# A graph layer and an expert layer in one kernel: one-hot tables from dst rows on ACT, and block results kept in DRAM until the edges are done

## The chip, the cores and the metric

The kernel runs on one core of a Trainium2 chip. The metric is the device time of one execution in microseconds (us), as the median of several runs. The core has five engines that matter here: PE (TensorE, matrix products; PEld is its weight load), DVE (VectorE), ACT (ScalarE), POOL (GpSimd) and SP (SyncE, which only issues DMAs). Each engine works through its own instructions in the order in which the program lists them. An instruction that has to wait holds up all that stands behind it on its engine, DMA issues included.

## The reference, cut to what matters

There are 6250 nodes with 256 features and 100,000 edges that are sorted by destination (`dst`), denser towards low node numbers. First a graph attention layer with 8 heads and a feed-forward net of 1024 hidden values, then a layer of 8 experts of which each token (node) takes two:

```python
h = (xn @ W).reshape(N, HEADS, HEAD_DIM)
e = jax.nn.leaky_relu(a_src[src] + a_dst[dst], NEG_SLOPE)
emax = jax.ops.segment_max(e, dst, num_segments=N)
ee = jnp.exp(e - emax[dst])
denom = jax.ops.segment_sum(ee, dst, num_segments=N)
alpha = ee / denom[dst]
msg = h[src] * alpha[:, :, None]
agg = jax.ops.segment_sum(msg, dst, num_segments=N)
out = agg.reshape(N, HEADS * HEAD_DIM) + xn @ W_res + bias
out = layer_norm(out, ln2_g, ln2_b)
ff = gelu_tanh(out @ ffn_w1 + ffn_b1) @ ffn_w2 + ffn_b2
x = x + out + ff
...
xe = xn[None, :, :] * ln_g[:, None, :] + ln_b[:, None, :]
h = jax.nn.gelu(jnp.einsum('end,edh->enh', xe, W1) + b1[:, None, :], approximate=False)
y = jnp.einsum('enh,ehd->end', h, W2) + b2[:, None, :]
y_tok = jnp.transpose(y, (1, 0, 2))
sel = jnp.take_along_axis(y_tok, top_idx[:, :, None], axis=1)
x = x + (weights[:, :, None] * sel).sum(axis=1)
```

Everything is in float32.

## The kernel before, in words

**First stage.** For 49 tiles of 128 nodes the kernel computes the attention tables and writes them to DRAM: `tab_s` (row per node: h and factors of the source) and `tab_q` (factors of the destination, 32 nodes in a row).

**Edges.** The edges are cut into tiles of 128. A step takes four tiles (G = 4), one from each of four windows; each window holds dst nodes of a range of 32. One to eight steps with the same windows are a group. There are 196 steps and 110 groups, and they run from the last nodes to the first (`order`, L285). A step passes through stages (`STAGES`, L910), each of which works a fixed number of steps behind the first:

- `fetch` (L806, step s): four indirect DMAs from POOL gather 4 x 128 rows of `tab_s` by source into `gs`.
- `spread` (L817, s): DVE compares each edge's place in its window with 0 to 31 and so makes the one-hot table `oh` (edge by node). At a group's first step it also makes `qd`, the factors of the group's 128 nodes in block-diagonal form, by multiplying `gd` with the constant `quad`.
- `turn_spread` (L832, one step later): PE transposes `oh` into the PSUM tile `pt`, and ACT copies it to `oht` (node by edge). `pt` has one buffer and is also used by `turn` (L960), which transposes the nets' inputs.
- `give` (L839, two steps later): PE multiplies `oht` with `qd`: each edge gets the factors of its destination, in `pz`.
- `weigh` (L846, three later): DVE makes the messages `msg` from `gs` and `pz`.
- `add_tiles` (L860, four later): PE sums the messages by node into `pl` with `oh` as weights; at a group's end ACT copies `pl` to `part`.
- `place` (L884, a group's end): DVE makes `oh2`, which shifts the group's 128 nodes to their place in two tiles of nodes; `add_nodes` (L891) multiplies with it on PE, and `sum_up` (L898) adds the product on DVE.

`fetch_nodes` (L787) gathers the destination factors of 32 groups at once, writes them to `tab_g` in DRAM and reads them back as `gd`, turned.

**Work beside the edges.** Between the stages of each step a planner (`run_tasks`, L937) puts tasks of the rest: 25 node units of two tiles (division by the sum, layer norm, net, residual, router) and blocks of the expert layer. A task has an engine and an estimated cost in us. A step has room on each engine (`ROOM`, L64), less what the edges need themselves (`EDGES`, `BEHIND` at a group's end); a task is put in when its engine has room left, and what it needs was put in one step or more before. PE's room beside edges is so 7.5 - 1.3 = 6.2. After the edges `ROOM_AFTER` holds. Tasks are made while less than 40 us (`QUEUE`) of PE work is waiting.

**Blocks.** When the router has done with a chunk of four node tiles, `rank` and `enlist` (L1274, L1298) give each token a slot in its experts' lists, and `scatter` (L1347) writes its normed row to `xs` by indirect DMAs from POOL. A block is 256 tokens of one expert. There are 53 (and some more that run only if needed). Which expert and where it starts is read from the lists at run time, and a block can be planned when the lists are sure to hold it (`sure`, L1387: tokens so far, times two, less 255 for each of the 8 experts, over 256). The last chunk is the single tile of the first 128 nodes. For a block SP loads the rows (`load_block`, L1401) and 2 MB of weights (`load_weights`, L1390, two buffers); `net` (L996) is 16 products `ph` with eight Gelu on ACT (`up`, L977) and 16 products `py` (`down`, L987), on PE with a cost of 15.4 us. `finish` (L1424) adds the bias on DVE into `yb` (two buffers), `weigh_block` (L1430) multiplies with the router's weights on ACT, and `give_back` (L1435) adds 2 x 128 rows to the output tensor in DRAM by two indirect DMAs from POOL. `note` (L1413) copies the rows' token numbers to `to` (three buffers).

`store_new` (L1091) writes the node units' rows to the same output tensor from SP. The framework puts a wait wherever two instructions touch the same tensor and one of them writes: each scatter-add waits for the landing of the one before.

The main loop is at L1483.

Of the kernel before, what the change touches and what calls it, by code (L numbers as in the profile page):

```python
# [40 lines left out]
F32 = mybir.dt.float32  # L42
# [22 lines left out]
EDGES = {"PE": 1.3, "DVE": 2.0}  # L65
BEHIND = {"PE": 0.5, "DVE": 1.4}
ROOM_AFTER = {"PE": 7.7, "DVE": 7.0, "ACT": 7.0, "POOL": 5.2, "SP": 1e9}
# [151 lines left out]
def gnn_moe_kernel(  # L219
# [68 lines left out]
    NCW = -(-NW // P)  # L288
    DUMMY = NP
# [29 lines left out]
    xt_d = dp.tile([NT, P, KD * P], F32, name="xt_d")  # L319
    xs = dp.tile([E * CAP + BT, DX], F32, name="xs")  # L320

# [12 lines left out]
    snloc = gp.tile([P, NQ], F32, name="snloc")  # L334
    here = gp.tile([P, 2, NQ], F32, name="here")
# [55 lines left out]

    quad = cp.tile([P, G], F32, name="quad")
    nc.vector.memset(quad, 0.0)
    for j in range(G):
        nc.vector.memset(quad[j * W32:(j + 1) * W32, j:j + 1], 1.0)
# [52 lines left out]
    with ExitStack() as actx:  # L448
# [96 lines left out]
        nc.vector.tensor_copy(srf, srow)  # L545
        ends = ap_.tile([P, 2, NCH], F32, name="ends")
# [69 lines left out]
        for j in range(G):  # L616
            q = slice(j * W32, (j + 1) * W32)
            nc.vector.tensor_scalar(sn[q], first[q, :, j], pcol[q], float(-j * W32), op0=ALU.add,
                                    op1=ALU.add)
        nc.vector.tensor_sub(sn, sn, kff)  # L620
        nc.vector.tensor_scalar(snloc, sn, float(P), float(-P), op0=ALU.is_ge, op1=ALU.mult)
        nc.vector.tensor_add(snloc, snloc, sn)
        nc.vector.tensor_sub(sn, first[:, :, 0], kff)
# [45 lines left out]

        nc.vector.memset(acc_hi[:, NT - KHI, :], 0.0)  # L670
# [100 lines left out]
    GC = P // G  # L771
# [13 lines left out]
    gds = {}  # L785

    def fetch_nodes(c):  # L787

        gq = bw.tile([P, W32 * 2 * H], F32, name="gq", bufs=1)
        nc.gpsimd.indirect_dma_start(  # L790
            out=gq, out_offset=None, in_=tab_q,
            in_offset=bass.IndirectOffsetOnAxis(ap=qrow[:, c:c + 1], axis=0))
        nc.sync.dma_start(tab_g[c * P:(c + 1) * P, :], gq)
        n = min(GC, NQ - c * GC)
        gd = bw.tile([P, GC, 2 * H], F32, name="gd")
        nc.sync.dma_start(gd[:, :n], tab_g[c * P:c * P + n * G, :].rearrange(
            "(g j) (r c) -> (j r) g c", j=G, r=W32))
        gds[c] = gd
# [18 lines left out]
    def spread(s):  # L817

        q, i = order[s]
        oh = bw.tile([P, G, W32], F32, name="oh", bufs=6)  # L820
# [4 lines left out]
        if i == 0:  # L825
            qd = bw.tile([P, G, 2 * H], F32, name="qd", bufs=3)
            gd = gds[q // GC][:, q % GC, :]
            nc.vector.tensor_tensor(qd, gd[:, None, :].to_broadcast([P, G, 2 * H]),
                                    quad[:, :, None].to_broadcast([P, G, 2 * H]), op=ALU.mult)
            live[q, "qd"] = qd  # L830

    def turn_spread(s):  # L832
        po = cps.tile([P, KD, 2 * P], F32, name="pt")
        nc.tensor.transpose(po[:, 0, :P], live[s, "oh"].rearrange("p j r -> p (j r)"), ident)  # L834
        oht = bw.tile([P, P], F32, name="oht")
        nc.scalar.activation(oht, po[:, 0, :P], AF.Copy)  # L836
        live[s, "oht"] = oht

    def give(s):  # L839

        pz = bps.tile([P, G * 2 * H], F32, name="pz", bufs=2)
        nc.tensor.matmul(pz, live.pop((s, "oht")), live[order[s][0], "qd"].rearrange(
            "p j c -> p (j c)"), start=True, stop=True)
        live[s, "pz"] = pz
# [39 lines left out]
    def place(q):  # L884

        oh2 = bw.tile([P, P], F32, name="oh2")
        nc.vector.tensor_scalar(oh2, jrow[:, :P], snloc[:, q:q + 1], None, op0=ALU.is_equal)
# [10 lines left out]
    def sum_up(q):  # L898
# [4 lines left out]
        for b in range(2):  # L903
# [6 lines left out]
    STAGES = ((sum_up, 6), (weigh, 3), (add_tiles, 4), (place, 4), (turn_spread, 1), (give, 2),  # L910
              (spread, 0), (add_nodes, 5), (fetch, 0))
# [312 lines left out]
    ebi = rp.tile([P, NB], I32, name="ebi")  # L1224
    endi = rp.tile([P, E], I32, name="endi")
# [187 lines left out]
    def note(b, env):  # L1413

        x = env["xb"]
        to = cw.tile([P, 2], I32, name="to", bufs=3)
        nc.vector.tensor_copy(to, x.bitcast(I32)[:, :, D])
# [4 lines left out]
        env["to"], env["wt"] = to, wt  # L1422
# [12 lines left out]
    def give_back(j, env):  # L1435
        nc.gpsimd.indirect_dma_start(  # L1436
            out=out, out_offset=bass.IndirectOffsetOnAxis(ap=env["to"][:, j:j + 1], axis=0),
            in_=env["yb"][:, j, :], in_offset=None, compute_op=ALU.add, bounds_check=N - 1,
            oob_is_err=False)
# [11 lines left out]
    def block_unit(b, env):  # L1451
# [8 lines left out]
        g0 = task(lambda: give_back(0, env), "POOL", 2.6, [wb_])  # L1460
        stored.append(task(lambda: give_back(1, env), "POOL", 2.6, [g0]))
# [15 lines left out]
    EARLY = 10  # L1477
    final_list, there = [], None
    s, u, since, was_nodes = 0, 0, [], False

    with tc.manual_schedule():
        nc.sync.dma_start(xs[E * CAP:, :].rearrange("(p r) d -> p r d", r=2), blank[:, :2])
        while s < NG + LASTST or pending or u < len(units) or len(blocks) < NS:  # L1483
            for g in range(s, min(s + EARLY, NG)):
                if order[g][0] // GC not in gds:
                    fetch_nodes(order[g][0] // GC)
# [3 lines left out]
            if s == NG + LASTST:  # L1490
                edges.close()
            if len(firsts) < len(units) and len(firsts) <= s + 1:
# [32 lines left out]
            run_tasks(s, room)  # L1525
            s += 1
# [43 lines left out]
```

## Time and profile before

| | us |
|---|---|
| median of 3 runs | 2186.42 (2183.76 to 2202.97) |
| the profiled execution's own time | 1972.14 |
| its span, first to last instruction | 1970.4 |
| busy: PE / PEld / DVE / ACT / POOL | 1634.8 / 1250.6 / 1078.1 / 707.7 / 1122.1 |
| mean granted clock of TensorE | 0.926 |
| last gather of edge rows starts | 1569.0 |
| last list of tokens scattered | 1711.2 |
| DMA | 348.24 MB, mean 177 GB/s |

The profiled execution took 214 us less than the median of the runs. Lines of the profile have the form: line of the code, engine, operation, out<-in by the program's names, shapes, count, then busy time and mean of one in ns, then the idle time ahead of it and who ended it. In lines of waits three numbers follow: us in total, times, longest. "issue" is time for which the profile shows no releaser. In the chain of waits each line has a start, a length and what it was. Windows give the busy us of each engine in a stretch. Matmul ends are modelled, so a busy PE is not PE at its peak. The span has three stages: up to about 137 us the tables, then 196 edge steps with other work beside them, and from about 1577 us blocks alone.

### The profile page before, as it was taken

To read this page: it belongs to the slowest core of one execution; us is meant where nothing else is said; L and a number is where in the kernel's file an instruction comes from. 1 tells how busy PE (TensorE), PEld (TensorE's weight loads), DVE (VectorE), ACT (ScalarE), POOL (GpSimd) and SP (SyncE) were. 2 spreads that over 40 slices of the span, in tenths; PEclk is the share of its full clock that TensorE was granted. 3 is DMA by queue.
4 is the path that set the end of the run, shared out by engine and by line. 5 is a ranking of instruction groups with operands and counts; after the bars stand their busy time and mean duration, and the time that the engine had idled before them with its cause. 6 is when DMAs were issued, how large, how long until landed. Compare 5 with 4: busy or idle time off the path is not lost. (4 is left out here: it accounts for less than half of the span.)

```text
span 1970.4 us, 28382 instructions
## 1 busy us (share of the span) xinstructions
PE 1634.8 (83%) x8533; PEld 1250.6 (63%) x8533; DVE 1078.1 (55%) x3964; ACT 707.7 (36%) x1590; POOL 1122.1 (57%) x1165
## 2 busy tenths in 40 slices
PE   4835797778787988999899997996998949999997
PEld 3523565555555766766677765775776737777775
DVE  8836878877878775565667655462453501200000
ACT  3821232322233343344434342433334314333332
POOL 2027765655655767577778777777777722112122
PEclk8968899887887999999999998998999979999999
DMA  4967664644535456566564776576776655565652
GB/s 129 290 210 225 187 202 130 184 134 146 158 112 194 152 152 170 149 199 168 179 200 136 210 206 200 155 220 201 201 232 169 205 184 131 179 186 171 196 161 57
DMA packets 245260, 348.24 MB, mean 177 GB/s; under 512 B 46465, under 2 KB 200353, under 8 KB 245100
## 3 DMA queue, kind: packets, MB, share of 16 engines
q1 hardware_dynamic: 182476, 203.56, 31.8%
q0 software_dynamic: 59312, 139.32, 27.1%
q10 hardware_dynamic: 3312, 3.48, 0.6%
q8 instruction: 70, 1.15, 0.2%
q14 instruction: 90, 0.74, 0.1%
HBM read 282.90 MB, written 67.66 MB: 178 GB/s over the span
## 5 line engine op out<-in xcount | busy, mean ns | idle before, releaser
L812 POOL DMA_INDIRECT gs<-tab_s,srce x784 | 809.9, 1033 | 363.9 <-issue 198.9
L981 PE MATMUL ph<-turned_in,w1b 128*128 128x256 f32 x1696 | 400.3, 390 | 51.2 <-ACT ht L984 38.2
L991 PE MATMUL py<-w2b,ht 128*128 128x256 f32 x1696 | 382.6, 384 | 11.7 <-DVE lg L1121 6.2
L981 PEld LDWEIGHTS ph<-turned_in,w1b 128*128 128x128 f32 x1696 | 305.2, 193 | 124.4 <-ACT ht L984 57.4
L991 PEld LDWEIGHTS py<-w2b,ht 128*128 128x128 f32 x1696 | 325.0, 193 | 58.4 <-DVE lg L1121 7.7
L1436 POOL DMA_INDIRECT out_dram<-yb,to x106 | 176.9, 1668 | 312.5 <-ACT yb L1432 124.5
L984 ACT ACTIVATE ht<-ph,pc 128x256 f32<-128x256 f32 x424 | 198.4, 473 | 206.1 <-PE ph L981 205.6
L854 DVE TENSOR_TENSOR msg<-gs,msg 128x1024 f32<-128x1024 f32 x196 | 240.5, 1227 | 6.7
L1426 DVE TENSOR_TENSOR yb<-py,b2b 128x512 f32<-128x512 f32 x53 | 36.6, 690 | 360.4 <-PE py L991 276.8
L991 PE MATMUL py<-w_sb,ht 128*128 128x256 f32 x784 | 190.5, 405 | 17.3 <-DVE lg L1121 15.0
L981 PE MATMUL ph<-turned_in,w_sb 128*128 128x256 f32 (+1 forms) x800 | 192.5, 394 | 14.2 <-ACT ht L984 14.2
L991 PEld LDWEIGHTS py<-w_sb,ht 128*128 128x128 f32 x784 | 158.7, 205 | 46.4 <-DVE lg L1121 19.6
L981 PEld LDWEIGHTS ph<-turned_in,w_sb 128*128 128x128 f32 x800 | 150.4, 200 | 44.6 <-ACT ht L984 20.3
L873 ACT ACTIVATE part<-pl 128x264 f32<-128x264 f32 x110 | 42.9, 390 | 322.3 <-PE pl L869 319.6
L836 ACT ACTIVATE oht<-pt 128x128 f32<-128x128 f32 x196 | 53.9, 275 | 271.5 <-PE pt L834 214.8
L869 PE MATMUL pl<-msg,oh 128*32 128x264 f32 x1568 | 130.9, 406 | 17.1 <-DVE msg L854 17.0
L1351 POOL DMA_INDIRECT xs<-xe,slot x98 | 103.4, 1055 | 54.3 <-DMA xs<-blank 22.1
L894 PE MATMUL p<-part,oh 128*128 128x264 f32 x220 | 84.3, 469 | 59.5 <-DVE acc_hi L905 38.8
L984 ACT ACTIVATE ht<-ph,prm 128x256 f32<-128x256 f32 (+1 forms) x200 | 92.2, 469 | 113.0 <-PE ph L981 112.6
L834 PEld LDWEIGHTS pt<-ident,oh 128*128 128x128 f32 x196 | 27.6, 141 | 138.3 <-issue 81.0
L834 PE MATMUL pt<-ident,oh 128*128 128x128 f32 x196 | 65.5, 334 | 49.6 <-ACT turned_in L973 23.1
L973 ACT ACTIVATE turned_in<-pt,pc 128x256 f32<-128x256 f32 x106 | 53.9, 559 | 134.4 <-PE pt L966 124.1
(325 smaller groups left out, 1900.8 us busy)
## 6 DMA issues: line engine op xcount, KB each, us to landing
w1b<-in_L_ffn_W_dram SPq DMA_DIRECT2D x53, 1024.0 KB
w2b<-in_L_ffn_W_dram SPq DMA_DIRECT2D x53, 1024.0 KB
xb<-xs SPq DMA_DIRECT2D x53, 260.0 KB
gs<-tab_s,srce POOLq DMA_INDIRECT x784, 3.3
b2b<-in_L_ffn_b_dram SPq DMA_DIRECT2D x53, 128.0 KB
tab_s<-hg SPq DMA_DIRECT2D x12, 544.0 KB
xg<-in_x_dram SPq DMA_DIRECT2D x12, 512.0 KB
xt_d<-xt SPq DMA_DIRECT2D x12, 512.0 KB
```

The costliest lines, as they stand in the source:

```text
L812: nc.gpsimd.indirect_dma_start(out=gs[:, j, :], out_offset=None, in_=tab_s, in_offset=bass.IndirectOffsetOnAxis(ap=srce[:, t:t + 1], axis=0))
L834: nc.tensor.transpose(po[:, 0, :P], live[s, "oh"].rearrange("p j r -> p (j r)"), ident)
L836: nc.scalar.activation(oht, po[:, 0, :P], AF.Copy)
L854: nc.vector.tensor_tensor(msg[:, :, :D].rearrange("p t (h d) -> p t h d", h=H), gs[:, :, :D].rearrange("p t (h d) -> p t h d", h=H), msg[: ...
L869: nc.tensor.matmul(pl[j * W32:(j + 1) * W32, :], oh[:, j, :], msg[:, j, :], start=i == 0, stop=last)
L894: nc.tensor.matmul(p2, oh2, part, start=True, stop=True)
L973: nc.scalar.activation(xt[:, k, :n * P], pt[:, k, :n * P], AF.Identity, bias=scale[:, KD + k:KD + k + 1], scale=scale[:, k:k + 1])
L981: nc.tensor.matmul(ph[:, :W], w1[:, k, c * P:(c + 1) * P], env["in"][:, k, :W], start=k == 0, stop=k == KD - 1)
L984: nc.scalar.activation(ht[:, :W], ph[:, :W], func, bias=b[:, c:c + 1], scale=1.0)
L991: nc.tensor.matmul(env["py"][:, j, :], env["ht", c][:, j * P:(j + 1) * P], w2[:, c, :], start=c == 0, stop=c == KF - 1)
L1351: st = nc.gpsimd.indirect_dma_start(out=xs, out_offset=bass.IndirectOffsetOnAxis(ap=slots[k][:n, t:t + 1], axis=0), in_=xes[u // 2][:n, pl ...
L1436: nc.gpsimd.indirect_dma_start(out=out, out_offset=bass.IndirectOffsetOnAxis(ap=env["to"][:, j:j + 1], axis=0), in_=env["yb"][:, j, :], in ...
```

## The change

**Tables by node.** `turn_spread` goes, and with it PE's transpose. The dst numbers are kept in DRAM in rows by tile (`dst_d`). For each step SP loads, two steps ahead (`load_dst`), the row of each of the four tiles' dst numbers to all 32 partitions of its window. ACT makes `oht` from it directly in two instructions (`is_node`): relu(1 - |dst - node|). The table `oh2` of `place` is made in the same way on ACT instead of by DVE, with its sign turned (`snloc`).

**Factors.** `qd` is no longer made on DVE for each group. Three tiles `qds`, cleared once, hold four groups each, and SP loads the factors into their diagonal blocks, four DMAs for four groups (`fetch_factors`). `quad` and `gd` go. The number of steps ahead at which nodes and factors are asked for is written anew.

**Blocks beside edges.** A block that is planned before step NG - 4 = 192 no longer gives back its result at once. ACT's queue writes `yb` to `ys` in DRAM (`put_by`). When the edges have ended and their buffers are closed, SP reads such results back into six buffers (`load_back`), one a step and at most three ahead, and POOL gives back one in a step if it has room (`backs`). Later blocks give back directly, as one task of cost 4.4 in place of two of 2.6.

**Scatter-adds.** The two of one block no longer wait for each other (an expert has a token once); those of different blocks still do. A small memset stands behind each, as it does in `scatter`. Token numbers stay in one tile `tos` for all blocks, in place of `to` with three buffers.

**Planner.** PE's own need beside edges is put at 0.95 in place of 1.3, DVE's at a group's end at 1.0 in place of 1.4; POOL's room after the edges at 6.0 in place of 5.2.

```diff
-EDGES = {"PE": 1.3, "DVE": 2.0}
-BEHIND = {"PE": 0.5, "DVE": 1.4}
-ROOM_AFTER = {"PE": 7.7, "DVE": 7.0, "ACT": 7.0, "POOL": 5.2, "SP": 1e9}
+EDGES = {"PE": 0.95, "DVE": 2.0}
+BEHIND = {"PE": 0.5, "DVE": 1.0}
+ROOM_AFTER = {"PE": 7.7, "DVE": 7.0, "ACT": 7.0, "POOL": 6.0, "SP": 1e9}
...
+    GC = 4
+    QB = 3
...
+    dst_d = dp.tile([NCH * P, P], F32, name="dst_d")
+    ys = dp.tile([NB, P, 2 * D], F32, name="ys")
...
+    node = gp.tile([P, NQ], F32, name="node")
+    qds = [gp.tile([P, GC, G, 2 * H], F32, name=f"qd{i}") for i in range(QB)]
...
+        nc.sync.dma_start(dst_d.rearrange("(c t) e -> t c e", t=P), drf)
...
+        nc.vector.tensor_scalar(node, sn, -1.0, None, op0=ALU.mult)
...
+        nc.vector.tensor_scalar(snloc, snloc, -1.0, None, op0=ALU.mult)
...
+        for qd in qds:
+            nc.vector.memset(qd, 0.0)
...
-        n = min(GC, NQ - c * GC)
-        gd = bw.tile([P, GC, 2 * H], F32, name="gd")
-        nc.sync.dma_start(gd[:, :n], tab_g[c * P:c * P + n * G, :].rearrange(
-            "(g j) (r c) -> (j r) g c", j=G, r=W32))
-        gds[c] = gd
+
+    def fetch_factors(c):
+
+        n = min(GC, NQ - c * GC)
+        for j in range(G):
+            nc.sync.dma_start(
+                qds[c % QB][j * W32:(j + 1) * W32, :n, j, :], bass.AP(
+                    tensor=tab_g.tensor,
+                    offset=tab_g.offset + (c * GC * G + j) * W32 * 2 * H,
+                    ap=[[2 * H, W32], [G * W32 * 2 * H, n], [1, 2 * H]]))
...
-        if i == 0:
-            qd = bw.tile([P, G, 2 * H], F32, name="qd", bufs=3)
-            gd = gds[q // GC][:, q % GC, :]
-            nc.vector.tensor_tensor(qd, gd[:, None, :].to_broadcast([P, G, 2 * H]),
-                                    quad[:, :, None].to_broadcast([P, G, 2 * H]), op=ALU.mult)
-            live[q, "qd"] = qd
-
-    def turn_spread(s):
-        po = cps.tile([P, KD, 2 * P], F32, name="pt")
-        nc.tensor.transpose(po[:, 0, :P], live[s, "oh"].rearrange("p j r -> p (j r)"), ident)
+
+    def load_dst(s):
+
+        q, i = order[s]
+        t0, m = groups[q]
+        rows_ = bg.tile([P, P], F32, name="rows_")
+        nc.sync.dma_start(rows_, bass.AP(tensor=dst_d.tensor, offset=dst_d.offset + (t0 + i) * P,
+                                         ap=[[m * P, G], [0, W32], [1, P]]))
+        live[s, "rows"] = rows_
+
+    def is_node(out, rows_, less):
+
+        nc.scalar.activation(out, rows_, AF.Abs, bias=less)
+        nc.scalar.activation(out, out, AF.Relu, bias=1.0, scale=-1.0)
+
+    def spread_by_node(s):
+
+        q, i = order[s]
         oht = bw.tile([P, P], F32, name="oht")
-        nc.scalar.activation(oht, po[:, 0, :P], AF.Copy)
+        is_node(oht, live.pop((s, "rows")), node[:, q:q + 1])
         live[s, "oht"] = oht
...
-        nc.vector.tensor_scalar(oh2, jrow[:, :P], snloc[:, q:q + 1], None, op0=ALU.is_equal)
+        is_node(oh2, jrow, snloc[:, q:q + 1])
...
-    STAGES = ((sum_up, 6), (weigh, 3), (add_tiles, 4), (place, 4), (turn_spread, 1), (give, 2),
-              (spread, 0), (add_nodes, 5), (fetch, 0))
+    STAGES = ((sum_up, 6), (weigh, 3), (add_tiles, 4), (spread_by_node, 1), (place, 4), (give, 2),
+              (spread, 1), (add_nodes, 5), (load_dst, -1), (fetch, 0))
...
-    def give_back(j, env):
-        nc.gpsimd.indirect_dma_start(
-            out=out, out_offset=bass.IndirectOffsetOnAxis(ap=env["to"][:, j:j + 1], axis=0),
-            in_=env["yb"][:, j, :], in_offset=None, compute_op=ALU.add, bounds_check=N - 1,
-            oob_is_err=False)
+    def give_back(b, yb):
+        for j in range(2):
+            st = nc.gpsimd.indirect_dma_start(
+                out=out, out_offset=bass.IndirectOffsetOnAxis(ap=tos[:, b, j:j + 1], axis=0),
+                in_=yb[:, j, :], in_offset=None, compute_op=ALU.add, bounds_check=N - 1,
+                oob_is_err=False)
+            tc.add_to_no_dep_group(f"block{b}", st.ins)
+            tc.declare_no_dep(st.ins, group=f"block{b}",
+                              reason="an expert has a token once, and what is no token nowhere")
+            nc.gpsimd.memset(between, 0.0)
+
+    def put_by(b, env):
+        nc.scalar.dma_start(ys[b].rearrange("p (j d) -> p j d", j=2), env["yb"])
+
+    def load_back(b):
+        yb = backp[0].tile([P, 2, D], F32, name="back")
+        nc.sync.dma_start(yb, ys[b].rearrange("p (j d) -> p j d", j=2))
+        return yb
...
-        g0 = task(lambda: give_back(0, env), "POOL", 2.6, [wb_])
-        stored.append(task(lambda: give_back(1, env), "POOL", 2.6, [g0]))
+        if s < NG - 4:
+            stored.append(task(lambda: put_by(b, env), "ACT", 0.05, [(wb_, 0)]))
+            put.append((b, stored[-1]))
+        else:
+            stored.append(task(lambda: give_back(b, env["yb"]), "POOL", 4.4, [wb_]))
...
             if s == NG + LASTST:
                 edges.close()
+                backp.append(gnn.enter_context(tc.tile_pool(name="back", bufs=6)))
...
             run_tasks(s, room)
+
+            if backs and backs[0][2] < s and room["POOL"] > 0:
+                give_back(*backs.pop(0)[:2])
+            if backp and put and put[0][1].step is not None and len(backs) < 3:
+                b = put.pop(0)[0]
+                backs.append((b, load_back(b), s))
             s += 1
```

More of the change, by code (lines that the diff above doesn't have):

```diff
@@ L390, in gnn_moe_kernel @@
     nc.gpsimd.iota(number, pattern=[[P, NT]], base=0, channel_multiplier=1)
[L392 to L395, printed above, removed]
     prm = cp.tile([P, NPR], F32, name="prm")
@@ L768, in gnn_moe_kernel @@
     fb2_bc = bcast(ffn_b2[None, :], "fb2_bc", D, fp)
-    GC = P // G
     cw = gnn.enter_context(tc.tile_pool(name="cw", bufs=2))
@@ L784, in gnn_moe_kernel @@
     live = {}
-    gds = {}
+    fetched = [0, 0]
     def fetch_nodes(c):
@@ L817, in spread @@
     def spread(s):
-        q, i = order[s]
-        oh = bw.tile([P, G, W32], F32, name="oh", bufs=6)
+        oh = bw.tile([P, G, W32], F32, name="oh", bufs=5)
         nc.vector.tensor_tensor(oh, jrow[:, None, :W32].to_broadcast([P, G, W32]),
@@ L841, in give @@
         pz = bps.tile([P, G * 2 * H], F32, name="pz", bufs=2)
-        nc.tensor.matmul(pz, live.pop((s, "oht")), live[order[s][0], "qd"].rearrange(
-            "p j c -> p (j c)"), start=True, stop=True)
+        q = order[s][0]
+        qd = qds[q // GC % QB][:, q % GC]
+        nc.tensor.matmul(pz, live.pop((s, "oht")), qd.rearrange("p j c -> p (j c)"), start=True,
+                         stop=True)
         live[s, "pz"] = pz
@@ L1224, in gnn_moe_kernel @@
     ebi = rp.tile([P, NB], I32, name="ebi")
+    tos = rp.tile([P, NB, 2], I32, name="tos")
     endi = rp.tile([P, E], I32, name="endi")
@@ L1415, in note @@
         x = env["xb"]
-        to = cw.tile([P, 2], I32, name="to", bufs=3)
-        nc.vector.tensor_copy(to, x.bitcast(I32)[:, :, D])
+        nc.vector.tensor_copy(tos[:, b], x.bitcast(I32)[:, :, D])
         wt = cw.tile([P, 2], F32, name="wt", bufs=3)
@@ L1421, in note @@
         nc.vector.tensor_add(wt, wt, x[:, :, D + 2])
-        env["to"], env["wt"] = to, wt
+        env["wt"] = wt
     def finish(env):
@@ L1477, in gnn_moe_kernel @@
     EARLY = 10
+    put, backs, backp = [], [], []
+    NCG = -(-NQ // GC)
     final_list, there = [], None
@@ L1482, in gnn_moe_kernel @@
         nc.sync.dma_start(xs[E * CAP:, :].rearrange("(p r) d -> p r d", r=2), blank[:, :2])
[L1483 to L1486, printed above, removed]
+        while (s < NG + LASTST or pending or u < len(units) or len(blocks) < NS
+               or put or backs):
+            while fetched[0] < NCW and order[min(s + EARLY, NG - 1)][0] // 32 <= NCW - 1 - fetched[0]:
+                fetch_nodes(NCW - 1 - fetched[0])
+                fetched[0] += 1
+            while (fetched[1] < NCG
+                   and order[min(s + EARLY - 4, NG - 1)][0] // GC <= NCG - 1 - fetched[1]):
+                fetch_factors(NCG - 1 - fetched[1])
+                fetched[1] += 1
+            if s == 0:
+                load_dst(0)
             for f, d in STAGES:
```

## The prediction

> **What bounds the kernel now.** I read the page first, then the windows of 100 us, the chain of waits in order of time, the waits by engine, and POOL's timeline after the edges. The page's first lines and groups:
>
> ```profile
> PE 1634.8 (83%) x8533; PEld 1250.6 (63%) x8533; DVE 1078.1 (55%) x3964; ACT 707.7 (36%) x1590; POOL 1122.1 (57%) x1165
> ...
> L1436 POOL DMA_INDIRECT out_dram<-yb,to x106 | 176.9, 1668 | 312.5 <-ACT yb L1432 124.5
> ...
> L836 ACT ACTIVATE oht<-pt 128x128 f32<-128x128 f32 x196 | 53.9, 275 | 271.5 <-PE pt L834 214.8
> ```
>
> PE is the busiest engine, and the work to be moved stands here: 196 turned tables (ACT's copy of each), 106 scatter-adds of block results on POOL (two for each of 53 blocks). The windows show two stages, one beside the edges and one after them:
>
> ```profile
> 1440.00:1570.00 130.00, 120.57 (x694) 92.31 (x693) 67.52 (x220) 52.96 (x115) 102.26 (x90) 1.00 0.70 203
> 1725.00:1955.00 230.00, 220.11 (x1024) 181.19 (x1023) 18.92 (x74) 83.97 (x180) 47.98 (x31) 1.00 0.54 162
> ```
>
> Columns after the length are busy us of PE, PEld, DVE, ACT, POOL, then clock, DMA share, GB/s. PE is busy for 93 to 96% in both. The last gather starts at 1569, the last edge product at 1591. In the second stage the chain of waits is PE alone, one block after the other:
>
> ```profile
> 1790.64 7.28 PE ph L981 x32
> 1797.92 6.91 PE py L991 x32
> 1804.83 0.45 PE pt L966 x4
> 1805.31 0.57 ACT turned_in L973
> ```
>
> From 1790.64 to the next such start at 1805.92 it is 15.28 us a block. Who waited for scatter-adds:
>
> ```profile
> DVE to L1417 <- DMA out_dram<-yb,to: 116.1, 17, 16.9
> ...
> DVE yb L1426 <- DMA out_dram<-yb,to: 69.3, 2, 43.7
> ...
> PE pt L834 <- ACT turned_in L973: 23.1, 42, 1.4
> ```
>
> (us in total, times, longest.) DVE, which works in order, stands 185 us behind scatters. PE hides most: its own timeline shows only three stops that follow from them, 10.2 us at 1227, 13.4 at 1368, 11.3 at 1624. Last, the pace of the scatters when nothing but themselves holds them:
>
> ```profile
> 1753.32 1.55 POOL L1436 DMA_INDIRECT out_dram<-yb,to  x1 [7.36 <-ACT yb L1432]
> 1758.29 1.55 POOL L1436 DMA_INDIRECT out_dram<-yb,to  x1 [3.42 <-DMA out_dram<-yb,to]
> 1766.22 1.55 POOL L1436 DMA_INDIRECT out_dram<-yb,to  x1 [6.39 <-ACT ht L984]
> 1773.31 1.55 POOL L1436 DMA_INDIRECT out_dram<-yb,to  x1 [5.54 <-issue]
> 1783.88 1.55 POOL L1436 DMA_INDIRECT out_dram<-yb,to  x1 [9.03 <-ACT yb L1432]
> ```
>
> POOL is busy 1.55 us and then stands 3 to 7 us until the sum has landed: each scatter adds into the same tensor and waits for the one before. The trace's median to landing here is 4.7 us. POOL's 21% busy share in this stage hides that its queue is taken for most of the time: from the first to the fourth scatter of two blocks pass 20.0 of their 30.6 us, and the fourth has still to land.
>
> **What the Trainium skill says.** (1) "ScalarE: Activation LUTs", section "What ACT_TABLE_LOAD costs": 186 ns + 0.833 ns an element, some 93 ns more for a per-partition operand; a 128x128 copy gives 293, the trace has 275. (2) The same page, "Table sets": relu and abs lie in every table set, so they reload nothing. The trace agrees for Copy and Identity (57 loads in the groups by line: 43 at Gelu, 13 at Exp, one at the start); for Abs and Relu no run here shows it. (3) "DMA: Bandwidth & Descriptors", "Anatomy of one DMA — SWDGE (gpsimd) path": most of the fixed 2 us is the wait for the write's receipt, and semaphores are waited for on the issuing sequencer, so POOL's whole queue stands. The trace agrees in kind, with 2.7 to 7.5 us. (4) "Trainium Kernel Development and Optimization", "Key Constraints": all queues share 16 DMA engines.
>
> **The change part by part**, in the profiled execution's time (span 1970.4 us).
>
> *Tables by node.* Removed are 196 transposes on PE. A row gives 334 ns, but they overlap: in the timeline the next product starts 0.165 us later (1302.90 to 1303.07). 196 x 0.165 = 32 us; bounds 32 and 65. Of the 23.1 us in which they wait for the shared PSUM tile I take half, 12; the next product waits for the same ACT result. Sum -44. ACT loses 196 x 0.275 and gains 196 + 110 pairs of Abs and Relu: estimate by the skill's price 387 + 293 = 0.68 us a pair, so +208 - 54 = +154 us. Its share in the edges goes from about 40 to 50%, covered by its waits for PE (318 us at L984 alone). But ht is queued behind a pair, and PE behind ht with two PSUM tiles: 0 to 0.3 us a step, I take 0.1, +20.
>
> DVE loses 110 x 0.218 (qd) + 110 x 0.282 (oh2) = 55 us. Up to 600 us (some 80% busy, and PE waits 58 us in all for its sums) a part counts: 0 to 35, I take -10. Small node operations, three clearings and dst_d's store come beside DVE and DMA work of the first 100 us: 0 to +3.
>
> *DMAs.* SP issues 196 row loads of 64 KB and 110 loads of factors; its issues take about 0.37 us, 113 us in all, on a queue that mostly waits. 12.5 MB beside 348 is nothing at a DMA share near 0.6. Rows are asked for two steps ahead (196 steps from 137 to 1577: 7.35 us each, 15 us); if late, ACT's whole queue stands (second rival).
>
> *Put by.* No scatter stands beside the edges any more. The stops at 1227 and 1368 go: -24. SP's waits for scatters at L1094 (264 us) go, hidden anyway. Each put-by costs ACT an issue, some 35 x 0.37 = 13 us, hidden.
>
> *Planner.* 0.95 for 1.3 admits 196 x 0.35 = 69 units more PE work beside the edges: +68 us there, and 4.5 blocks (of 15.36 units) fewer after. So the edges end at 1577 - 44 + 20 - 10 - 24 + 68 = about 1587.
>
> *After the edges.* By scatters, 29 blocks were through before 1577 (58 scatters); now about 33.5 are computed, and with those planned ahead some 35 put by. Ahead of the last, single tile the lists cover (2 x 6122 - 8 x 255) / 256 = 39 blocks, which caps it. All their scatters come now, beside those of the 18 other blocks: 53 pairs after about 1605 (last edge product 1601, then the edge buffers close and a load of 2 to 4 us) where 24 were before. A pair does not wait inside: two busy times and the gap as at L1351, 1.55 + 0.31 + 1.55 = 3.4 us. The next block still waits for both landings. First-to-second distances of the 24 pairs after 1600 average 5.57 us, a wait of 4.0; all chain-held ones between 1753 and 1945 average 4.7. I take 4.3, so 7.7 us a block; bounds 2.94 (the shortest regular wait: 6.35) and 5.6 (9.0). 52 x 7.7 = 400 us; 1605 + 400 + 8 for the last pair to land = 2013.
>
> PE would need less: the last list came 134 us after 1577, of which 25 were a stop that goes in part, so 1587 + 109 = 1696, 18 more until the first of its blocks starts (1711 to 1729), 14 x 15.28 = 214, tail 10: 1938. So POOL sets the end by 75 us. The stall then shows up so: yb has two buffers, an own block's scatters stand behind read-back ones, finish on DVE waits for yb, py on PE for finish. The last tokens' scatters into xs (1709 before) queue behind them too.
>
> So +43 us, all from the stage after the edges. **On the median**: the profiled execution took 1972.14 us, the runs 2186.42, 214 more, and no view says where. If all stretches, +43 becomes +48; if only PE's part does (edges and blocks, 11%), the second stage of before (393 us) gains 43 and the scatters nothing, which leaves 0. I take the middle, +24: 2210.
>
> **Rivals.** *The queue keeps pace.* For it: landings of 2.9 us occur whenever no weights are loaded (1887 to 1964), and slower blocks load less. Against: 5 to 6 us while they are. From 6.2 us a block and less, (1938 - 10 - 1605) / 52, PE and the last list set the end: 1938 - 1970 = -32, 2154; with the upper price of the transposes and no delay on ACT 2110. The sign turns at 6.9 us, (1970 - 8 - 1605) / 52.
>
> *Rows come late.* SP waits 197 us at L1404 for scatters into xs between 700 and 1600, 10 times, longest 34.1; ten waits, 4.6 us on average over two steps' 15, would cost 46 us more in the edges: 2256. Against: SP runs ahead of its steps, and a wait that starts early harms nobody.
>
> *Table loads.* If Abs or Relu did reload, 306 pairs x 2 x 1.283 us (the trace's load) = 785 us more on ACT, about +300. Against: the skill's statement.
>
> **How the numbers follow.** Scatters set the end: 0.55 (2186 to 2275 as its own range). They keep pace: 0.32. Rows late: 0.10. Table loads: 0.03. A measurement of this kernel can tell about 1% from no change, 22 us. Of the first case 0.12 lies within it, of the second 0.05, of the third 0.01. Faster 0.27, same 0.18, slower 0.55. The range 2110 to 2290 takes the second case in whole and the first up to about 9 us a block (1605 + 468 + 8 = 2081, +111, less the 19 of the stretch: 2278).
>
> **What would show it.** Right: POOL's timeline after the edges has pairs 1.9 us apart and then a wait of 3 to 6, without rest; DVE yb waits for out_dram there; PE below 85% busy from 1600 to 1900; no L834; the waits at L1417 gone; edges ending near 1587. Wrong: PE at 95% after the edges, the span under 1950, or many waits of ACT for rows; pairs of different blocks following each other without a landing between them would fell the sum.

## The result, and the profile after

The changed kernel takes 2299.34 us (median of 4 runs, 2286.95 to 2305.28) where the kernel before takes 2188.78 (4 runs, 2183.76 to 2202.97): 1.0487 times as long, 95% interval 1.0419 to 1.0554. The forecast was 2210 with a range to 2290: the direction was right, and the rise of 111 us is more than four times the 24 forecast.

One thing has to be known to read the numbers below. The same kernel before takes about 1975 us in some comparisons (kernels timed together) and about 2190 in others, and the profile shown ahead of the prediction (1972.14) was of the first sort while the timed runs were of the second; so a time is compared only with times of its own comparison, and "beside 1975" and "beside 2190" name the sort. For the profile of after (span 2303.4) the fitting one of before is that of a further run with a span of 2198.2.

The page of after, busy us and the groups that the change made or touched:

```profile
PE 1739.5 (76%) x8337; PEld 1307.4 (57%) x8337; DVE 1041.0 (45%) x3744; ACT 841.4 (37%) x2002; POOL 1104.9 (48%) x1271
...
L1449 DVE TENSOR_TENSOR yb<-py,b2b 128x512 f32<-128x512 f32 x53 | 36.6, 691 | 472.2 <-DMA out_dram<-yb,tos 221.4
...
L1460 POOL DMA_INDIRECT out_dram<-back,tos x66 | 103.2, 1564 | 145.0 <-issue 89.8
...
L1460 POOL DMA_INDIRECT out_dram<-yb,tos x40 | 62.5, 1563 | 133.7 <-ACT yb L1455 57.5
```

196 matmuls are gone and ACT has 134 us more to do. Of the 53 blocks 33 were put by (66 scatters from `back`), 20 gave back straight from `yb`. DVE's idle time before `yb` is led by landings of scatters, 221 us. Where that idle time lies, the windows show. Stretches after the edges, of after (last edge product at 1844.8):

```profile
1845.00:1900.00 55.00, 50.27 (x243) 42.17 (x240) 11.35 (x50) 25.26 (x54) 18.41 (x22) 0.97 0.73 208
1900.00:2000.00 100.00, 63.52 (x280) 52.43 (x279) 15.13 (x80) 25.84 (x53) 44.17 (x55) 0.81 0.68 169
2000.00:2100.00 100.00, 61.46 (x249) 49.67 (x249) 5.44 (x20) 19.42 (x42) 43.64 (x52) 0.80 0.68 156
2100.00:2210.00 110.00, 71.81 (x292) 57.65 (x292) 5.03 (x20) 24.33 (x52) 49.54 (x59) 0.83 0.61 140
2210.00:2303.00 93.00, 78.81 (x367) 64.79 (x365) 6.28 (x22) 28.95 (x62) 24.28 (x30) 0.97 0.39 116
```

and of the fitting profile of before (last edge product at 1826.1):

```profile
1900.00:2000.00 100.00, 94.85 (x448) 78.88 (x447) 19.65 (x102) 36.97 (x77) 19.32 (x15) 1.00 0.60 179
2000.00:2100.00 100.00, 95.41 (x446) 78.17 (x444) 8.59 (x32) 36.97 (x79) 20.11 (x13) 1.00 0.62 181
```

The number after the length of the stretch is PE's: 95% before, 61 to 65% after over 310 us. 196.8 us of work in 310 where 95% would be 294.5: PE does nothing for 98 us that it did not lose before. No engine is near full in these stretches. POOL's timeline of after shows what is (its small memsets, which overlap the scatters, left out):

```profile
1892.04 1.56 POOL L1460 DMA_INDIRECT out_dram<-back,tos  x1 [2.37 <-DMA out_dram<-back,tos]
...
1904.72 1.56 POOL L1460 DMA_INDIRECT out_dram<-back,tos  x1 [2.81 <-issue]
...
1906.59 1.56 POOL L1460 DMA_INDIRECT out_dram<-back,tos  x1 [0.19 <-issue]
...
1911.07 1.56 POOL L1460 DMA_INDIRECT out_dram<-back,tos  x1 [2.82 <-issue]
...
1912.93 1.56 POOL L1460 DMA_INDIRECT out_dram<-back,tos  x1 [0.19 <-issue]
```

The two scatters of a block start 1.87 us apart; then the next block's pair waits until both have landed (1906.59 to 1911.07: 4.48 us). The profile names the landing at some of the pairs, as at 1892.04, and no releaser at others; that it is the landing there too, an experiment below shows. From the first pair at 1858.49 to the 45th at 2200.33 it is 341.8 us, 7.77 a pair on average (single distances from 5.9 to 12.1). How such a landing holds PE is in the chain of waits of after, in order of time (start, us, what):

```profile
2195.93 3.66 DMA out_dram<-yb,tos
...
2199.78 0.70 DVE yb L1449
...
2200.97 0.49 ACT yb L1455
2201.46 0.37 ACT ht L1007
2201.87 6.89 PE ph L1004 x24
2208.76 6.92 PE py L1014 x32
```

A block's scatter lands, its `yb` buffer comes free, DVE finishes the next block into it, ACT goes on to `ht`, and only then PE starts. Last, the end of POOL's timeline, when the read-backs are through:

```profile
2233.12 1.56 POOL L1460 DMA_INDIRECT out_dram<-yb,tos  x1 [4.29 <-ACT yb L1455]
...
2255.86 1.56 POOL L1460 DMA_INDIRECT out_dram<-yb,tos  x1 [19.19 <-ACT yb L1455]
...
2263.69 1.56 POOL L1460 DMA_INDIRECT out_dram<-yb,tos  x1 [4.29 <-ACT yb L1455]
...
2286.42 1.56 POOL L1460 DMA_INDIRECT out_dram<-yb,tos  x1 [19.19 <-ACT yb L1455]
```

Here POOL waits for blocks and not blocks for POOL: two blocks (2233.12 to 2263.69) in 30.6 us, the 15.3 a block of PE alone.

The stage after the edges so has 13.7 us until the first pair, 341.8 of chain, 93.4 of the last eight blocks (2200.33 to 2293.69) and 9.7 to the end: 458.6 us. Before it has 372.1 (1826.1 to 2198.2).

### The profile page after: what moved, and what is told of

Read it like the earlier page. It is cut to its first block, busy times and chain, and to the rows that moved or that the text cites. A ratio compares the mean times of both kernels' runs of the same rounds, so it can differ in the third digit from the quotient of the medians.

```text
span 2303.4 us, 28723 instructions
## 1 busy us (share of the span) xinstructions
PE 1739.5 (76%) x8337; PEld 1307.4 (57%) x8337; DVE 1041.0 (45%) x3744; ACT 841.4 (37%) x2002; POOL 1104.9 (48%) x1271
## 5 line engine op out<-in xcount | busy, mean ns | idle before, releaser
L826 POOL DMA_INDIRECT gs<-tab_s,srce x784 | 792.2, 1010 | 741.2 <-DVE oh L834 466.1
L1004 PE MATMUL ph<-turned_in,w1b 128*128 128x256 f32 x1696 | 439.4, 415 | 145.1 <-ACT ht L1007 95.1
L1004 PEld LDWEIGHTS ph<-turned_in,w1b 128*128 128x128 f32 x1696 | 330.3, 207 | 237.1 <-ACT ht L1007 115.5
L1004 PE MATMUL ph<-turned_in,w_sb 128*128 128x256 f32 (+1 forms) x800 | 222.8, 437 | 73.4 <-ACT ht L1007 54.7
L1449 DVE TENSOR_TENSOR yb<-py,b2b 128x512 f32<-128x512 f32 x53 | 36.6, 691 | 472.2 <-DMA out_dram<-yb,tos 221.4
L1004 PEld LDWEIGHTS ph<-turned_in,w_sb 128*128 128x128 f32 x800 | 169.7, 225 | 115.0 <-ACT ht L1007 62.4
L1014 PE MATMUL py<-w_sb,ht 128*128 128x256 f32 x784 | 190.8, 403 | 11.8 <-DVE lg L1144 4.7
L892 PE MATMUL pl<-msg,oh 128*32 128x264 f32 x1568 | 146.0, 434 | 36.6 <-ACT part L896 21.4
L1460 POOL DMA_INDIRECT out_dram<-back,tos x66 | 103.2, 1564 | 145.0 <-issue 89.8
L865 PEld LDWEIGHTS pz<-qd,oht 128*128 128x128 f32 x392 | 64.7, 207 | 128.5 <-issue 115.0
L928 DVE SCALAR_TENSOR_TENSOR acc_lo<-p,here,acc_lo 128x264 f32 x112 | 55.2, 493 | 161.0 <-PE p L917 72.9
L1460 POOL DMA_INDIRECT out_dram<-yb,tos x40 | 62.5, 1563 | 133.7 <-ACT yb L1455 57.5
```

The costliest lines, as they stand in the source:

```text
L826: nc.gpsimd.indirect_dma_start(out=gs[:, j, :], out_offset=None, in_=tab_s, in_offset=bass.IndirectOffsetOnAxis(ap=srce[:, t:t + 1], axis=0))
L865: nc.tensor.matmul(pz, live.pop((s, "oht")), qd.rearrange("p j c -> p (j c)"), start=True, stop=True)
L892: nc.tensor.matmul(pl[j * W32:(j + 1) * W32, :], oh[:, j, :], msg[:, j, :], start=i == 0, stop=last)
L928: nc.vector.scalar_tensor_tensor(to, p2, here[:, b, q:q + 1], to, op0=ALU.mult, op1=ALU.add)
L1004: nc.tensor.matmul(ph[:, :W], w1[:, k, c * P:(c + 1) * P], env["in"][:, k, :W], start=k == 0, stop=k == KD - 1)
L1014: nc.tensor.matmul(env["py"][:, j, :], env["ht", c][:, j * P:(j + 1) * P], w2[:, c, :], start=c == 0, stop=c == KF - 1)
```

## The experiments

The theory to test was: the chain of scatters, which put-by moves behind the edges, costs the time, and neither the tables nor the planner's numbers do. Rivals: ACT's pairs of instructions a table delay the edges; the new numbers crowd the edges; the stage after would be long even without the chain, because of what the planner moved. In each table the last edge product is the last of `add_tiles` (`pl`) in the profiled run, and the stage counts from there to its end; the times are medians. All versions keep the pairs that don't wait inside, `tos` and SP's loads of factors.

**Nothing put by, and each other part undone (beside 1975).** One more profile of the kernel before serves this comparison:

> The kernel before once more, for a profile whose own time is near its runs' median (the first profiled execution took 1972 us, the runs 2188). Both theories expect some 2190 us. If the extra time is PE's granted clock (0.926 in the first profile), the clock is near 0.86 here and the edges end near 1577 x 1.11 = 1750; the stage after the edges is then 393 x 1.11 = 436 us. If it is spread evenly over all engines, single instructions of ACT and DVE are longer too.

It took 1972.67 us, so it is of the faster sort and says nothing of the extra time.

Nothing put by; everything else as after:

```diff
-        if s < NG - 4:
+        if s < 0:
```

> The changed kernel, but no block is put by: each gives its result back when it is done, two scatter-adds that don't wait for each other. My theory (the changed kernel loses its time in the stage after the edges, where 53 pairs of scatters go one after the other): the stage from the last edge product to the end falls from 458 to some 370 us, and the time from 2299 to about 2200. Rival 1 (the edges are slower, by ACT's tables and rows from SP): 2270 or more, since the edges stay as they are; even slower if SP's stores wait for scatters again and hold up the rows.

Put-by and the new numbers, but tables by PE's transpose and ACT's copy as before, `oh2` on DVE (the order of the stages goes back with it, and no rows are loaded):

```diff
-        oht = bw.tile([P, P], F32, name="oht")
-        is_node(oht, live.pop((s, "rows")), node[:, q:q + 1])
+        po = cps.tile([P, KD, 2 * P], F32, name="pt")
+        nc.tensor.transpose(po[:, 0, :P], live[s, "oh"].rearrange("p j r -> p (j r)"), ident)
+        oht = bw.tile([P, P], F32, name="oht")
+        nc.scalar.activation(oht, po[:, 0, :P], AF.Copy)
...
-        is_node(oh2, jrow, snloc[:, q:q + 1])
+        nc.vector.tensor_scalar(oh2, jrow[:, :P], snloc[:, q:q + 1], None, op0=ALU.is_equal)
```

> The changed kernel, but the tables are made as before: PE's transpose, ACT's copy, oh2 on DVE, no rows from SP. Put-by and the planner's numbers stay as changed. My theory: PE gets 32 to 65 us more work, so 2299 to 2350. Rival 1 (ACT's pairs ahead of ht, and rows that come late, lengthen the edges): the edges' end falls from 1845 by 60 us or more, and the time to 2240 or less.

Put-by and the tables, but the planner's old numbers:

```diff
-EDGES = {"PE": 0.95, "DVE": 2.0}
-BEHIND = {"PE": 0.5, "DVE": 1.0}
+EDGES = {"PE": 1.3, "DVE": 2.0}
+BEHIND = {"PE": 0.5, "DVE": 1.4}
```

with 5.2 for POOL's room after the edges in place of 6.0.

> The changed kernel with the planner's numbers of before (PE 1.3, DVE 1.4, POOL 5.2). My theory: fewer blocks beside the edges, the edges end about 68 us earlier, as much more work after them, where PE waits for scatters anyway (62% busy): 30 to 70 us faster, about 2250. Rival (the numbers are right, PE being the bound): 2300 to 2340.

Two runs of a later comparison of the same sort belong here: put-by alone, which takes both edits above (transposes and old numbers), and after itself.

> Put-by with transposes and the planner's numbers of before: the part that is missing in the table of combinations. If put-by is what makes the change slower, this alone is 1.03 to 1.05 of before; the stage after the edges is longest here, 490 us or so, since more blocks are left for it, and the edges end earlier than in the kernel before by 30 to 50 us.

> The changed kernel beside them. 1.049 of before where before takes about 2185 us; where it takes about 1974, the last edge product near 1590 and 450 to 460 us more, 1.035 of before.

Measured:

| kernel | us | ratio to before | last edge product | stage after |
|---|---|---|---|---|
| before (one run) | 1972.67 | | 1584.3 | 386.6 |
| nothing put by | 1942.10 | 0.9824 [0.9786, 0.9861] | 1615.3 | 331.1 |
| put-by + new numbers | 2039.30 | 1.0331 [1.0306, 1.0356] | 1582.0 | 455.9 |
| put-by + tables | 2047.49 | 1.0362 [1.0337, 1.0388] | 1551.5 | 494.3 |
| put-by alone | 2046.24 | 1.0377 [1.0349, 1.0405] | 1552.2 | 489.1 |
| all (after) | 2046.79 | 1.0388 [1.0356, 1.0421] | 1582.0 | 455.2 |

The other runs of before took 1974.59 in the first of the two comparisons and 1975.38 in that of the last two rows. Read down the last two columns. Put-by alone shortens the edges by 32 us (1584.3 to 1552.2) and lengthens the stage after by 102. The tables move neither column by more than a few us. The planner's numbers move 30 us from the stage after into the edges and leave the end where it was. Two expectations missed: transposes were to cost up to 50 us and the old numbers to bring 30 to 70, and both versions lie within 8 us of after (2046.79). Without put-by the stage after takes 331 us, and this kernel, which keeps tables, numbers and pairs, is the only version here that is faster than before, by less than 2%, and it is not so beside 2190 (below). Its stage beside that of after, in windows that leave out the last stretch (nothing put by, then after):

```profile
1615.00:1940.00 325.00, 302.76 (x1431) 249.93 (x1430) 42.22 (x191) 123.80 (x263) 75.89 (x92) 1.00 0.56 163
```

```profile
1582.00:1940.00 358.00, 245.10 (x1047) 199.80 (x1040) 37.14 (x169) 92.80 (x197) 153.08 (x184) 0.84 0.68 166
```

PE 93% against 68%, POOL 76 us against 153.

**The chain cut in two (beside 2190).** After itself again, and after with the scatter-adds of every second block going into another DRAM tensor, so that blocks that follow each other often need not wait for each other. The output lacks the share of these blocks; the amount of work is the same.

```diff
-                out=out, out_offset=bass.IndirectOffsetOnAxis(ap=tos[:, b, j:j + 1], axis=0),
+                out=res_d if b % 2 else out,
+                out_offset=bass.IndirectOffsetOnAxis(ap=tos[:, b, j:j + 1], axis=0),
```

> The changed kernel itself, beside the others, since the kernel before takes 1974 us in this comparison where it took 2188 in the first. If the loss is mostly waiting of a fixed length (scatters), the ratio to before is above 1.0487 where PE runs faster, some 1.05 to 1.06 and 2080 us. If it is PE's and ACT's time, it stays near 1.049 (2071). The last edge product at some 1640, and 400 us or more from there to the end.

> The changed kernel, but the results of odd blocks are added into another tensor in DRAM (that of the residual products, which is no longer needed by then), so that a pair of scatters waits only for the last pair of its own parity. The odd blocks' share is missing from the output. If the wait of a pair for the landing of the pair before it sets the stage after the edges, a block there costs some 4 us of POOL instead of 8 and the stage is bound by PE: 100 us or more faster than the changed kernel, near 1960. If reading back, SP's order or DMA traffic set it, less than 30 us.

After took 2297.25 us (1.0487 [1.0423, 1.0550]), two sums 2193.33 (1.0014 [0.9985, 1.0043]). Its stage after the edges is 357.0 us (1841.3 to 2198.3), a pair comes every 5.36 us, and PE is back at its share:

```profile
1900.00:2000.00 100.00, 93.85 (x436) 77.37 (x435) 16.82 (x83) 38.47 (x80) 62.59 (x76) 0.98 0.96 251
```

POOL's timeline of this run shows why: pairs into the two tensors follow each other with no landing between, and only the third waits.

```profile
1962.26 1.56 POOL L1460 DMA_INDIRECT out_dram<-back,tos  x1 [0.19 <-issue]
...
1964.12 1.57 POOL L1460 DMA_INDIRECT out_dram<-back,tos  x1 [0.19 <-DMA back<-ys]
...
1968.87 1.56 POOL L1460 DMA_INDIRECT res_d<-back,tos  x1 [3.06 <-DMA res_d<-yb,tos]
...
1970.73 1.57 POOL L1460 DMA_INDIRECT res_d<-back,tos  x1 [0.19 <-issue]
...
1972.61 1.56 POOL L1460 DMA_INDIRECT out_dram<-yb,tos  x1 [0.19 <-issue]
```

DVE's wait at `yb` for landings falls from 221.4 us to 61.3 (42.0 for `res_d`, 19.3 for the output). The same scatters, the same writes and read-backs, 104 us less: it is the waiting of one sum for the other that costs, not the DMAs nor POOL's instructions. This settles the main question.

**Parts without put-by (beside 2190).** Three ways, each with the put-by undone as above: the new numbers without tables, the tables without the new numbers, and neither (only the pairs that don't wait, `tos` and SP's loads of factors are left). Nothing put by with both, before and after ran once more as well. The first two expectations were written for a kernel before of 1974 us; it took 2185.44 there.

> Blocks give back at once, tables by transposes, with the changed planner's numbers (and factors loaded by SP, pairs without a wait inside). Tables and rows are thus taken out of the version without put-by, which took 1942. My sum gives tables by node 32 to 65 us less of PE and 20 more by ACT: 1955 to 1985 here. If ACT's tables cost more than they bring, below 1942.

> Blocks give back at once, tables by node on ACT, the planner's numbers of before. Taken from the version that took 1942, only the planner's numbers go back. By my sum (work moved from one full stage of PE to another) 1935 to 1950; if the smaller need of PE is what fills the steps, 1960 to 1975.

> Blocks give back at once, tables by transposes, the planner's numbers of before: what remains of the change is that the two scatters of a block don't wait for each other, token numbers without buffers to wait for, and factors loaded by SP. By my sum the stops of PE behind scatters (24 us beside the edges, 11 after) go in part: 0.985 to 1.0 of before. If these stops are only moved to the next wait, 1.0.

> The changed kernel, but blocks give back at once. 0.98 of before where before takes about 1974 us, as measured. Where before takes about 2185: if tables and numbers together bring what neither brought alone there (1.009 and 1.010), 0.99 or less; if they bring nothing there, 1.00 to 1.01.

> The kernel before, for its trace beside those of this comparison. If before takes about 2185 us here, the edges end near 1820 and about 365 us follow, as in the versions that give back at once (1832 and 363 us with tables by node alone); so the stage after the edges, not the edges, holds the difference of the changed kernel (1840 and 459). If it takes about 1974, the trace is that of the first profile (1584 and 387).

> The changed kernel. Near 1.049 of before if before takes about 2185 us. If before takes about 1974: the edges end near 1590 (as with planner and put-by), 440 to 460 us follow, 2040, a ratio of 1.03 to 1.04.

The first two ratios are to a before of 2185.44, the others to one of 2187.94.

| kernel | us | ratio to before | last edge product | stage after |
|---|---|---|---|---|
| before | 2200.02 (one run; others 2187.94) | | 1826.1 | 372.1 |
| numbers, nothing put by | 2206.21 | 1.0104 [1.0051, 1.0157] | 1869.9 | 332.1 |
| tables, nothing put by | 2206.76 | 1.0091 [1.0052, 1.0130] | 1831.5 | 364.3 |
| neither, nothing put by | 2198.74 | 1.0068 [1.0042, 1.0093] | 1829.2 | 363.7 |
| both, nothing put by | 2226.22 (2192.64 to 2231.09) | none given | 1888.4 | 334.1 |
| all (after) | 2295.57 | 1.0496 [1.0421, 1.0571] | 1824.8 | 457.8 |

Each part alone costs about 1% or less here. With both, three runs lay at 2224 to 2231 and one at 2192.64; that is inconclusive, but no gain as in the other sort of comparison. What stands in both sorts: put-by adds 124 us to the stage after (331.1 to 455.2, and 334.1 to 457.8) and takes 33 and 64 us off the edges (1615.3 to 1582.0, and 1888.4 to 1824.8).

**Fewer blocks put by (beside 1975).** Only blocks planned before step 110 of 196:

```diff
-        if s < NG - 4:
+        if s < 110:
```

> The changed kernel, but only blocks planned before step 110 are put by (about a dozen in place of 33). If the stage after the edges is long because 44 pairs of scatters in a row cost 7.7 us each while PE has the work of 20 blocks, then 12 read-back pairs beside 20 own ones, 32 x 7.7 = 246 us, fit under PE's time: the stage is back at 335 to 345 us from 458, and the time 80 us or more below that of the changed kernel. If the mere reading back costs, the stage stays above 380.

1976.59 us, 1.0008 [0.9997, 1.0020]: 11 read-backs in place of 33, the last edge product at 1607.5, the stage after 368.1. The pairs come at 7.90 us each while read-backs last (1627.7 to 1738.3), after which PE sets the pace. The stage is 87 us shorter than after's and the edges 25 longer. So the drain costs about in proportion to what is put by: a third of the read-backs leave the stage 37 us longer than with nothing put by (331.1), where all 33 leave it 124 longer. The expectation that these few would fit under PE's time (335 to 345 us) missed.

**Tables on DVE in place of ACT.** Tables alone (old numbers, nothing put by), with one DVE instruction a table:

```diff
-        is_node(oht, live.pop((s, "rows")), node[:, q:q + 1])
+        nc.vector.tensor_scalar(oht, live.pop((s, "rows")), node[:, q:q + 1], 0.0, op0=ALU.add,
+                                op1=ALU.is_equal)
```

and `oh2` in the same way; first beside 1975, then together with the one on ACT, beside 2196.

> Tables by node from dst rows, planner's numbers of before, nothing put by, as in the version with tables alone (1.009 where before took 2185), but made on DVE in one instruction (add, is_equal) in place of two on ACT. If ACT's pairs ahead of ht eat what PE saves on transposes, 20 to 45 us faster than tables alone. If PE's saving is itself small (0.165 us a transpose or less, or hidden), within 10 us of it.

> Tables by node on ACT, the planner's old numbers, nothing put by, beside a version with the same tables on DVE on the same chip. If ACT's two instructions a table delay ht and so take back what the missing transposes give, this one is slower than the one on DVE by 0.5 to 1.5% and ACT is waited for longer by PE (PE ph for ACT ht about 118 us against 40 to 80). If not ACT but the later start of the edges and the longer way of the dst rows take it back, the two are within 0.4% of each other.

> The same with each table by one instruction on DVE. ACT delays: 0.5 to 1.5% under the one on ACT, at or below the kernel before. Start and rows: within 0.4% of it.

1973.02, 0.9990 [0.9972, 1.0008] in the first. In the second the tables on ACT took 2209.89, 1.0056 [1.0029, 1.0082], and those on DVE 2227.37, 1.0132 [1.0078, 1.0186]. In the profiles of the second the last edge product comes at 1829.2 with ACT, 1860.6 with DVE, and 1829.2 came out above with transposes. That is neither of the two outcomes expected. Taking the tables off ACT so doesn't bring the missing gain: where both ran together, the time went up. It isn't shown that ACT's load costs nothing, since DVE got the work in its place. The version on ACT has no higher ratio than the one with transposes (1.0068). One place where the tables by node come late is seen, at the start. Before, the first edge product with factors:

```profile
142.75 0.53 PE L842 MATMUL pz<-qd,oht 128*128 128x64 f32 x2
```

After, by SP's queue, ACT and PE:

```profile
142.99 5.82 SPq L808 DMA_DIRECT2D qd<-tab_g  x12
149.12 0.45 SPq L844 DMA_DIRECT2D rows__1862<-dst_d  x1
```

```profile
152.65 0.40 ACT L850 ACTIVATE oht<-rows__1862,node 128x128 f32<-128x128 f32 x1 [29.43 <-DMA rows__1862<-dst_d]
```

```profile
153.49 0.66 PE L865 MATMUL pz<-qd,oht 128*128 128x64 f32 x2 [32.03 <-DMA xtf<-xt_d]
```

Twelve loads of factors are issued ahead of the first row, and the first product comes 10.7 us later (142.75 to 153.49). With transposes but factors by SP it starts at 145.1 to 150.6 in the four profiles, so the factors are a part of this. But the delay doesn't last: the product of the seventh step starts at 188.2 in after and at 189.8 in this profile of before, and beside 1975 at 184.5 and 181.3. What the missing transposes should have given is not found; see below.

## Why the prediction was wrong

**Right: what sets the end.** "So POOL sets the end": the pairs, the wait behind each (7.77 us a pair measured on average, 7.7 forecast, from landings in before), DVE's waits at `yb`, PE under 85% and no stops for scatters in the edges are all in the trace, and cutting the chain takes 104 us away. 33 blocks were put by, 35 were forecast.

**Wrong: the length of the drain** ("52 x 7.7 = 400 us; 1605 + 400 + 8"). The prediction counts from the last product of `add_nodes`, put at 1601, which makes 412 us; in after that product is at 1846.6, and the rest took 456.8 (453.3 beside 1975). Term by term: 11.9 us to the first pair in place of 4, +8; 44 pairs at 7.77 in place of 7.7, +3; the last eight own blocks 93.4 us in place of 8 x 7.7 = 62, +32; 9.7 in place of 8 at the end, +2. Together +45. The working compared two chains, POOL's 2013 and PE's "PE would need less ... 1938", and took the longer. They don't run beside each other. With two `yb` buffers each own block waits for its turn in POOL's queue behind read-backs, so PE does 12 blocks in 349 us (1858 to 2207) where 15.3 us each allow 22; when the read-backs are through, eight blocks are left, and these go at PE's pace. The text named this stall and left it out of its sum. Here the slow queue ahead of the fast engine adds the engine's remaining work at the end. What more `yb` buffers would change wasn't tried.

**Wrong: from the profile to the median** ("if only PE's part does ... the second stage of before gains 43 ... I take the middle"). This took 19 us off. In the profile of before of the slower sort the stage after isn't stretched at all: 372.1 us against 386.6. All the extra time lies in the edges (last product at 1826.1 against 1584.3). Nothing of the loss could be hidden there.

**The edges' end** (+10 forecast, by "1577 - 44 + 20 - 10 - 24 + 68"): -2 us beside 1975 and +19 (1826.1 to 1844.8) in the two profiles beside 2190, by `add_tiles`; by `add_nodes`, as the prediction counts, -8 and +13. About right as a sum beside 2190, by other parts. Tables: -34 forecast, less than 1 us found (1552.2 to 1551.5, and 1582.0 in both). Planner: +68 forecast, +30 found (+57 without put-by, beside 2190). Scatters gone from the edges: -24 forecast, -32 found.

The sum for the two profiles beside 2190: 24 forecast, +45 drain, +19 stretch, +3 edges (13 in place of 10), +14 because the stage of before, counted from `add_nodes`, was 364.6 us there and not the 379 of its first profile (1591 to 1970): 105, as measured (2303.4 - 2198.2).

**The rivals.** "The queue keeps pace" fell: a pair took 7.77 us, and its limit was 6.2. It shows up with two sums (5.36 us a pair), and then the change is worth nothing either way. "Rows come late": ACT waits for a row once in the profile of after, the 29.4 us at the start, and four times, 11.8 us in all, in that beside 1975. "Table loads": 39, 13 and 1 in the groups by line in place of 43, 13 and 1, none at L850 or L851; Abs and Relu reload nothing, as the Trainium skill says ("ScalarE: Activation LUTs", "Table sets").

**ACT's price** was right: 386 ns for the Abs of `oh2` and 310 for its Relu, 0.70 us a pair where 0.68 was worked out from the Trainium skill ("ScalarE: Activation LUTs", "What ACT_TABLE_LOAD costs": 387 and 293).

**Open.** Why 196 transposes less on PE bring nothing: neither the waits for rows nor the later start, which is soon made up, explains it, and the tables on DVE didn't bring it either. Why nothing put by is 1.8% faster beside 1975 and not beside 2190. And why the two sorts of comparison differ. TensorE's granted clock was at half speed for 246 us up to the edges' end in the further profile of before of the faster sort (1584.3), and for 471 in the one that ended the edges at 1826.1; but 225 us more at half speed lose at most 113 of the 242 us between. The traces show one more difference. In the slower sort ACT and DVE have waits whose end the profile can put to no instruction ("remote"): none in the nine profiles of the faster sort, 344 to 542 us in each of the eleven of the slower, all before the edges end. In the profile of before of the slower sort 337.7 of the 343.6 us are waits for PE's semaphore. One of them:

```profile
1210.64 0.28 ACT L836 ACTIVATE oht<-pt 128x128 f32<-128x128 f32 x1 [3.45 <-remote]
```

The transpose that this copy reads ends at 1207.52 by PE's record, 3.1 us earlier. This points to PE's products being ready later than its records say in these edges, so PE's busy time there can't be taken at its word. What makes it so wasn't tried.

## What to carry to other kernels

Work that is held back until a stage has ended comes out as a queue, so price it at the pace of that queue, and ask what stands in line behind it: with few buffers the busiest engine is held to the queue's pace and does its own work afterwards, so the two times add in part where a maximum of both was expected. Here scatter-adds into one tensor cost a landing a pair, whatever the busy share says. Beside the edges they cost 33 or 64 us, put by and done afterwards 124; a second tensor to sum into took away nearly all of the loss (1.0014 against 1.0487). Before a profile's time is carried over to the runs' median, look which stage of the slower runs is longer.

## What was not expected of the hardware

TensorE's granted clock was lower where PE had less to do: 0.80 at 61% busy (2000 to 2100 of after) and 1.00 at 95% (the same stretch of before), and 0.84 at 68% against 1.00 at 93% beside 1975. PE stands idle for 32 to 39% of the two stretches at the low clock, so a low clock is no proof of a hard-worked PE. And one kernel had two times 11% apart, 1972 and 2190: all the difference lies in its edges, more time at half clock goes with it, and that accounts for half of it at most.
